# Product 3 of a sparse layer stack: rows gathered for three units at the start, then for the unit three ahead

## The chip, the cores and the metric

One Trainium2 chip, one of its cores. The metric is the device time in microseconds (us) of one execution; the lower the better. Beside it, one further execution was taken with the hardware profiler, and the views quoted below come from that one.

## The reference, cut to what matters

Four graph layers on 4096 nodes with 128 features share one adjacency matrix, and each ends in a residual sum and a layer norm. The matrix is sparse (about 0.2% of its entries are not zero), but it is given dense, as 64 MB of float32. The change lies in layer 1, a Chebyshev layer made of two convolutions with two products each by the matrix:

```python
def cheb_conv(x, L, W, b):
    Tx0 = x
    out = Tx0 @ W[0]
    Tx1 = L @ x
    out = out + Tx1 @ W[1]
    Tx2 = 2.0 * (L @ Tx1) - Tx0
    out = out + Tx2 @ W[2]
    return out + b
h = elu(cheb_conv(x, L, W0, b0))
h = elu(cheb_conv(h, L, W1, b1))
```

## The kernel before, in words

The adjacency matrix stays in HBM. It is read as chunks of 1 MB (4 x 128 rows by 512 columns) on SyncE's DMA queue, line 145, into a pool of five buffers. A product by the matrix is, for a block of 512 columns, eight chunks with four matmuls each (`propagate`, line 722, the matmul at line 730).

Layer 1 has four such products. They need the matrix four times over, and loading and multiplying it costs TensorE and DMA time. So the kernel finds the non-zero entries of each row while the chunks pass, and makes lists of them (`Lists.build`, line 1405, on VectorE). With a finished list a block of 512 result rows can be computed another way: the needed rows of the right-hand side are gathered one index per partition from a table in HBM, and weighed and summed on chip. In product 3 (`L @ h` with `h` already multiplied by a weight, called `v`), the blocks `PAIRED = [0, 1, 2]` are done that way, and the five blocks 3 to 7 are done densely by `propagate`.

The gathered part of product 3 is cut into 12 units of 128 result rows (`third_product`, line 1660). For a unit u:

- `pull(u)`, line 1665, takes a buffer `got3` of a pool with three buffers and issues nine gathers (`rows_of`, line 1543), each an indirect DMA on GpSimd of 128 rows of 512 bytes. Behind each stands `pause`, a multiplication of one column (line 1563). Both are tied, by `keep_in_program_order` (line 1518), behind the instruction written before them on GpSimd. That tie sets an order in GpSimd's queue and no wait for another engine.
- `weigh(u)`, line 1670, on ScalarE and VectorE: it scales the unit's own rows (line 1551), makes three one-hot matrices `hot` (line 1553) and adds six of the nine gathered rows, weighed, to `here` (line 1556).
- `product(u)`, line 1676, on TensorE: three matmuls of `hot` by the other three gathered rows (line 1682), two by a weight (line 1684), then the sum into `w` on VectorE (line 1685). In the kernel before, `pull(u + 2)` is written behind it.

When these are written is set by a plan with hooks: one hook for each of the 40 dense chunks. `weigh(u)` is written at hooks 6, 9, 11, 14, 16, 19, 22, 24, 27, 30, 32 and 35, and `product(u)` one hook later. At hooks 0 to 4 and at every odd one a step of `build` for the lists of blocks 3 to 7 is written (line 1715). Behind product 11, at hook 36, stand 24 gathers of list values (`values`, line 1521), and behind these on GpSimd the gathers for the next product (line 2006).

The order in which engines carry out what is written is, up to the end of product 3, set by the compiler's planner: on each engine it takes the instruction that is ready first by its own reckoning of durations, and among the ready ones the one written first. Exceptions are tied: gathers and pauses on GpSimd as said, and on VectorE everything of `build` and `weigh` in the order written (`chained`, line 1379). A new tile in a pool of three buffers waits at its first write for the last reader of the tile that had the buffer before. From `sparse_layers` (line 1722) on, the order on TensorE, VectorE, ScalarE and GpSimd is the order written.

Of the kernel before, what the change touches and what calls it, by code (L numbers as in the profile page):

```python
# [46 lines left out]
def adj_resnorm_d4(ctx: ExitStack, tc: tile.TileContext, x_in, xT_in, adj, adjT, pairs, diag_in, w0g, w0gT, a0, w1a, b1a,  # L47
# [633 lines left out]
    def network(usual):  # L681

        with ExitStack() as whole:
# [3 lines left out]
            with ExitStack() as first, ExitStack() as l1h_pool:  # L687
# [123 lines left out]
                if usual:  # L811
                    fetch(PAIRED[-1], TB * 9)
                    lists.paired(PAIRED[-1])
                    l1s = l1h_pool.enter_context(tc.tile_pool(name="l1s", bufs=2, reuse_waits="tile"))
                    third = third_product(lists, l1s, ps_tr, ps_mm, v, w, hT, W1B, wd, h0T)
# [774 lines left out]
    def tile_of(u):  # L1590
        return PAIRED[u // TB] * TB + u % TB
# [68 lines left out]
    def third_product(lists, pool, ps_tr, ps_mm, v, w, hT, W1B, wd, h0T):  # L1660
        units = len(PAIRED) * TB
        E = NEAR + QT
        got, made = {}, {}

        def pull(u):
            if u < units:
                got[u] = pool.tile([P, E, F], F32, name="got3", bufs=3)
                deque(lists.rows_of(u, got[u], 0), 0)

        def weigh(u):  # L1670
            here = pool.tile([P, F], F32, name="here3")
            hot = pool.tile([P, QT, P], F32, name="hot3")
            lists.weigh(u, v[:, tile_of(u), :], got[u], here, hot, True)
            made[u] = here, hot

        def product(u):
            t = tile_of(u)
            here, hot = made.pop(u)
            g = got.pop(u)
            p = ps_tr.tile([P, F], F32, name="ptr")  # L1680
            for j in range(QT):
                nc.tensor.matmul(p, hot[:, j, :], g[:, j, :], start=j == 0, stop=False)
            for hh in range(hT.shape[1]):
                nc.tensor.matmul(p, hT[:, hh, t * P:(t + 1) * P], W1B[:, hT.shape[1] + hh, :], start=False, stop=hh == hT.shape[1] - 1)
            nc.vector.tensor_tensor(w[:, t, :], p, here, ALU.add)
            pull(u + 2)
            if u % TB == TB - 1:
                c = PAIRED[u // TB]
                blk = slice(c * IB, (c + 1) * IB)
                lists.store(1, c, w)  # L1690
                ph = ps_mm.tile([P, IB], F32, name="pmm")
                for hh in range(hT.shape[1]):
                    nc.tensor.matmul(ph, wd[:, hh, :], hT[:, hh, blk], start=hh == 0, stop=hh == hT.shape[1] - 1)
                nc.scalar.copy(h0T[:, blk], ph)

        def builds():
            for c in (3, 4, 5, 6, 7):
                for _ in lists.build(c, True):
                    yield

        build = builds()
        pull(0)
        pull(1)
        plan = {}
        for u, h in enumerate((6, 9, 11, 14, 16, 19, 22, 24, 27, 30, 32, 35)):
            plan.setdefault(h, []).append(lambda u=u: weigh(u))
            plan.setdefault(h + 1, []).append(lambda u=u: product(u))
        plan[36].append(lambda: (deque(lists.values(3), 0), deque(lists.values(4), 0)))
        hooks = [0]

        def seen(ib, n, c, a):
            h = hooks[0]
            hooks[0] += 1
            if h < 5 or h % 2:
                next(build, None)
            for f in plan.pop(h, ()):
                f()
            if h == 39:
                assert not plan and next(build, None) is None
        return seen  # L1720
# [436 lines left out]
```

## Time and profile before

| what | value |
|---|---|
| time, median of 3 runs | 1839.98 us (1831.49 to 1844.66) |
| the profiled execution, its own time | 1653.07 us |
| its span, first to last instruction | 1651.2 us |
| granted TensorE clock, mean over the span | 0.95 |
| busy: TensorE, VectorE, GpSimd, ScalarE | 90%, 69%, 50%, 23% |
| product 3, about 808 to 1000 us: TensorE, VectorE, GpSimd busy | 181.19, 152.57, 147.74 of 192 us |
| HBM read | 404.39 MB, 253 GB/s with what is written |

The profiled execution was 187 us shorter than the median of the plain runs. It is one execution, and the page doesn't show a plain one; positions and durations below are those of the profiled execution.

Engines are called PE (TensorE), PEld (its weight loads), DVE (VectorE), ACT (ScalarE), POOL (GpSimd) and SP (SyncE). A line of the timeline has the start in us, the duration in us, engine, source line, operation, what is written and read, the count of merged instructions, and in brackets how long the engine sat idle before it and what released it ("issue": nothing that the profile shows). The trace writes `got` for the tile `got3` and `rows` for the table. The matmuls of float32 are recorded as two instructions each, so that three matmuls are "x6".

### The profile page before, as it was taken

To read this page: it belongs to the slowest core of one execution; us is meant where nothing else is said; L and a number is where in the kernel's file an instruction comes from. 1 tells how busy PE (TensorE), PEld (TensorE's weight loads), DVE (VectorE), ACT (ScalarE), POOL (GpSimd) and SP (SyncE) were. 2 spreads that over 40 slices of the span, in tenths; PEclk is the share of its full clock that TensorE was granted. 3 is DMA by queue.
4 is the path that set the end of the run, shared out by engine and by line. 5 is a ranking of instruction groups with operands and counts; after the bars stand their busy time and mean duration, and the time that the engine had idled before them with its cause. 6 is when DMAs were issued, how large, how long until landed. Compare 5 with 4: busy or idle time off the path is not lost.

```text
span 1651.2 us, 16460 instructions
## 1 busy us (share of the span) xinstructions
PE 1478.5 (90%) x4744; PEld 714.2 (43%) x4744; DVE 1138.4 (69%) x3203; ACT 385.5 (23%) x693; POOL 833.1 (50%) x1322
## 2 busy tenths in 40 slices
PE   6899999999999999999999999889927689788886
PEld 3344444544444444454444454444413344444444
DVE  5987655789887897988699950455336756556766
ACT  5776540010000011121200000222223111122234
POOL 0000000000242188848486888888648888888841
PEclk9999999999999999999999999999967798889988
DMA  9867776588888885867587888778665677678673
GB/s 374 342 256 301 246 271 233 179 277 299 316 315 320 309 285 195 281 210 274 177 296 248 291 278 305 252 265 287 241 151 153 189 259 244 219 239 278 218 192 95
DMA packets 106972, 419.30 MB, mean 254 GB/s; under 512 B 21556, under 2 KB 44088, under 8 KB 67064
## 3 DMA queue, kind: packets, MB, share of 16 engines
q1 hardware_dynamic: 59984, 360.01, 61.1%
q0 software_dynamic: 22656, 36.17, 8.6%
q10 hardware_dynamic: 24232, 21.98, 4.5%
q8 instruction: 39, 0.64, 0.2%
q14 instruction: 61, 0.50, 0.1%
HBM read 404.39 MB, written 13.70 MB: 253 GB/s over the span
## 4 chain that ended last, share of the span: by engine, by line
PE 46%; DVE 25%; POOL 14%; issue 6%; DMA 6%; ACT 3%; ACTq 0%; DVEq 0%; POOLq 0%
PE pacc L730 15%; PE pacc L423 12%; POOL got L1820 6%; PE pp L2050 5%; DMA got<-table,source 4%; PE pp L1931 3%; POOL got L1518 3%; DVE at L1397 3%; DVE top L1396 2%; POOL idle L1563 2%; DVE here L1556 1%; POOL value L1518 1%; DVE same L1317 1%; DVE gw L1856 1%; DVE acc L1944 1%
## 5 line engine op out<-in xcount | busy, mean ns | idle before, releaser
L1820 POOL DMA_INDIRECT got<-table,source x288 | 275.8, 958 | 88.8 <-issue 62.0
L1931 PE MATMUL pp<-chunk,xT 128*128 128x512 f32 x496 | 244.0, 633 | 1.4 <-ACT xT L1902 0.7
L730 PE MATMUL pacc<-chunk,x 128*128 128x512 f32 x512 | 222.6, 593 | 0.0
L1518 POOL DMA_INDIRECT got<-rows,source x180 | 182.8, 1016 | 67.6 <-issue 38.6
L423 PE MATMUL pacc<-chunk,hw 128*128 128x512 f32 x408 | 188.7, 607 | 0.8 <-DVE hw L466 0.7
L1358 POOL IOTA i<- 128x384 int32 (+3 forms) x4 | 1.0, 238 | 345.7 <-PE pden L411 329.8
L2050 PE MATMUL pp<-chunk,w 128*128 128x512 f32 x384 | 173.1, 600 | 0.0
L730 PE MATMUL pacc<-chunk,t 128*128 128x512 f32 x384 | 171.5, 597 | 0.0
L730 PEld LDWEIGHTS pacc<-chunk,x 128*128 128x128 f32 x512 | 96.0, 190 | 114.7 <-issue 114.6
L730 PE MATMUL pacc<-chunk,v 128*128 128x512 f32 x320 | 144.5, 597 | 0.0
L1396 DVE MAX8 top<-chunk 128x8 f32<-128x512 f32 x196 | 128.5, 677 | 14.1 <-DMA chunk<-in_adjT 14.1
L1931 PEld LDWEIGHTS pp<-chunk,xT 128*128 128x128 f32 x496 | 94.2, 203 | 91.2 <-issue 84.1
L1397 DVE FIND_INDEX8 at<-top,chunk 128x8 uint16<-128x512 f32 x196 | 133.1, 684 | 0.0
L1518 POOL DMA_INDIRECT both_ways<-in_pairs,both_at x108 | 106.6, 987 | 17.4 <-issue 17.1
L423 PEld LDWEIGHTS pacc<-chunk,hw 128*128 128x128 f32 x408 | 75.0, 192 | 92.1 <-issue 86.3
L1563 POOL TENSOR_TENSOR idle<-idle 128x1 f32<-128x1 f32 x489 | 110.3, 226 | 8.6
L730 PEld LDWEIGHTS pacc<-chunk,t 128*128 128x128 f32 x384 | 71.7, 192 | 81.8 <-issue 81.8
L2050 PEld LDWEIGHTS pp<-chunk,w 128*128 128x128 f32 x384 | 71.7, 194 | 78.5 <-issue 77.7
L395 ACT ACTIVATE junk<-chunk 128x2048 fp8e4<-128x2048 f32 x51 | 97.4, 1910 | 29.8 <-DMA chunk<-in_adjT 29.3
L329 DVE TENSOR_SCALAR pos<-chunk 128x2048 bf16<-128x2048 f32 x66 | 80.1, 1219 | 33.7 <-DMA chunk<-in_adjT 32.1
L1863 PE MATMUL u<-gw,into 128*128 128x132 f32 x192 | 33.2, 317 | 68.3 <-DVE gw L1856 68.3
L1556 DVE SCALAR_TENSOR_TENSOR here<-got,back,here 128x128 f32<-128x128 f32 x120 | 42.2, 352 | 67.0 <-DMA got<-rows,source 63.8
(424 smaller groups left out, 2058.7 us busy)
## 6 DMA issues: line engine op xcount, KB each, us to landing
chunk<-in_adjT SPq DMA_DIRECT2D x326, 1024.0 KB, 5.4
keep<-in_adjT SPq DMA_DIRECT2D x13, 1024.0 KB, 11.0
spread<-spread ACTq DMA_DIRECT2D x16, 384.0 KB, 4.5
got<-table,source POOLq DMA_INDIRECT x288
chunk<-in_adjT ACTq DMA_DIRECT2D x4, 1024.0 KB
got<-rows,source POOLq DMA_INDIRECT x180
table<-rows ACTq DMA_DIRECT2D x8, 264.0 KB, 5.2
xT<-in_xT ACTq DMA_DIRECT2D x8, 256.0 KB, 6.5
```

The lines of the kernel that those rows point to most:

```text
L329: r = nc.vector.tensor_scalar(pos, a, 0.0, None, op0=ALU.is_gt)
L395: nc.scalar.activation(junk, a, AF.Relu, scale=-1.0, accum_out=bad[:, n:n + 1], saturate=False)
L423: in_order(nc.tensor.matmul(p, hw[:, j * TB + k, :], a[:, k, :], start=first and k == 0, stop=last and k == TB - 1))
L730: nc.tensor.matmul(p, stationary(c * TB + k), a[:, k, :], start=n == 0 and k == 0, stop=n == NB - 1 and k == TB - 1)
L1396: pin(nc.vector.max(self.top[:, t, ib, :], row))
L1397: pin(nc.vector.max_index(self.at[:, t - TB, ib, :], self.top[:, t, ib, :], row))
L1518: tc.keep_in_program_order(nc.gpsimd.indirect_dma_start(out, None, of, bass.IndirectOffsetOnAxis(ap=index, axis=0)))
L1556: pin(nc.vector.scalar_tensor_tensor(here, got[:, j, 0:F], self.back[:, u, j:j + 1], here, op0=ALU.mult, op1=ALU.add))
L1563: return nc.gpsimd.tensor_tensor(self.idle[:, 0:1], of, self.idle[:, 1:2], ALU.mult)
L1820: nc.gpsimd.indirect_dma_start(got[t][:, j, :], None, table, bass.IndirectOffsetOnAxis(ap=lists.source[:, t, j:j + 1], axis=0))
L1931: nc.tensor.matmul(p, y[:, t0 + k, :], a[:, ib % (TB // n), k, :], start=k == 0, stop=k == n - 1)
L2050: nc.tensor.matmul(p, w[:, c * TB + k, :], a[:, k, :], start=n == 0 and k == 0, stop=n == NB - 1 and k == TB - 1)
```

## The change

At its beginning product 3 pulls the rows of units 0, 1 and 2 and not only of units 0 and 1; behind product u it pulls those of unit u + 3 and not of unit u + 2. The pool keeps its three buffers, `pull` still does nothing for a unit past the last, and the hooks, the lists and the number of gathers (108) stay.

```diff
@@ third_product, product(u)
             nc.vector.tensor_tensor(w[:, t, :], p, here, ALU.add)
-            pull(u + 2)
+            pull(u + 3)
             if u % TB == TB - 1:
@@ third_product
         build = builds()
-        pull(0)
-        pull(1)
+        for u in range(3):
+            pull(u)
         plan = {}
```

## The prediction, made before the changed kernel was run

> **What bounds the kernel now.** I read the page first, for the shares of the engines and for the rows of the gathers:
>
> ```profile
> span 1651.2 us, 16460 instructions
> ...
> PE 1478.5 (90%) x4744; PEld 714.2 (43%) x4744; DVE 1138.4 (69%) x3203; ACT 385.5 (23%) x693; POOL 833.1 (50%) x1322
> ...
> L1518 POOL DMA_INDIRECT got<-rows,source x180 | 182.8, 1016 | 67.6 <-issue 38.6
> ```
>
> TensorE is busy for 90% of the span, so over the whole it is the bound. The gathers on POOL take 1.016 us each, without the pause behind them. Then I asked for busy times by stage, of product 3 (808 to 1000 us) and of the begin of the next product (to 1110 us):
>
> ```profile
> 808.00:1000.00 192.00, 181.19 (x582) 87.00 (x581) 152.57 (x551) 12.74 (x26) 147.74 (x231) 1.00 0.80 272
> 1000.00:1110.00 110.00, 98.17 (x285) 48.34 (x284) 38.71 (x130) 17.55 (x33) 95.10 (x166) 0.95 0.80 273
> ```
>
> The columns are: the stretch, its length, then busy us and counts of PE, PEld, DVE, ACT and POOL, the clock, the DMA share and GB/s. PE leaves 192 - 181.19 = 10.8 us idle in product 3 and 110 - 98.17 = 11.8 us after it, and that is all that a better supply of rows could give back to PE there. The chain of waits for the same stretch puts POOL's gathers first (17.2% "POOL got L1518", 7.5% "POOL value L1518"), and it follows POOL without a gap from 965.77 us, a gather of product 3, to 1072.23 us, a gather of the next product. So POOL's stream does set when the rows arrive at the end of this stage. A gap in that stream before 965 us is not free.
>
> So the third view was the timeline of POOL, for the gaps, and beside it that of PE and DVE for who reads the buffers. First POOL:
>
> ```profile
> 855.18 0.97 POOL L1518 DMA_INDIRECT got<-rows,source  x1 [0.15 <-issue]
> 856.54 0.97 POOL L1518 DMA_INDIRECT got<-rows,source  x1 [0.15 <-DVE high L1317]
> 857.53 0.20 POOL L1563 TENSOR_TENSOR idle<-idle 128x1 f32<-128x1 f32 x1
> 861.02 0.97 POOL L1518 DMA_INDIRECT got<-rows,source  x1 [3.29 <-PE pacc L730]
> ...
> 872.06 1.20 POOL L1518 DMA_INDIRECT got<-rows,source  x1 [0.15 <-issue]
> 873.27 0.29 POOL L1563 TENSOR_TENSOR idle<-idle 128x1 f32<-128x1 f32 x1
> 886.10 0.97 POOL L1518 DMA_INDIRECT got<-rows,source  x1 [12.53 <-issue]
> ```
>
> and the first three products on PE and weighings on DVE, which are units 0, 1 and 2:
>
> ```profile
> 857.63 1.00 PE L1682 MATMUL ptr<-got,hot 128*128 128x128 f32 x6 [0.54 <-DVE hot L1553]
> 882.71 1.00 PE L1682 MATMUL ptr<-got,hot 128*128 128x128 f32 x6
> 890.00 0.83 PE L1682 MATMUL ptr<-got,hot 128*128 128x128 f32 x6
> ```
>
> ```profile
> 858.01 2.28 DVE L1556 SCALAR_TENSOR_TENSOR here<-got,back,here 128x128 f32<-128x128 f32 x6
> 883.08 2.28 DVE L1556 SCALAR_TENSOR_TENSOR here<-got,back,here 128x128 f32<-128x128 f32 x6
> ```
>
> The first gather of product 3 starts at 816.16 us. Counting nine to a unit, unit 0 is 816.16 to 829.43, unit 1 starts at 830.79, unit 2 at 843.00 and has its ninth at 856.54, unit 3 starts at 861.02 and has its ninth at 872.06, unit 4 starts at 886.10. What decides this case is to lay these starts beside the products behind which the pulls are written. Pull 2 is written behind product 0, but its first gather started at 843.00, 14.6 us before product 0 (857.63). Pull 3 is written behind product 1 (882.71) and started at 861.02, 21.7 us before it. Pull 4 is written behind product 2 (890.00) and started at 886.10. So the written place does not hold a gather back. What holds it is its buffer: unit 3 needs that of unit 0, whose last reader on DVE ended at 858.01 + 2.28 = 860.29, and the gather came 0.73 us later. Unit 4 needs that of unit 1, read until 883.08 + 2.28 = 885.36, and came 0.74 us later. Unit 2 found the third buffer free, since nobody had used it, and followed unit 1 with the usual 0.15 us.
>
> **What the Trainium skill says.** "PSUM — Partial Sum Buffer", section "Engine vs sequencer instructions", says that the queues of ScalarE, VectorE and GpSimd are strictly first in, first out. The trace agrees: while the first gather of unit 4 waits 12.53 us, nothing else runs on POOL. "DMA: Bandwidth & Descriptors", section "Issuing engine by pattern", gives indirect transfers to GpSimd, and its section "Latency and other measured facts" puts the first byte of a transfer from there at about 1 us; here the gather's instruction itself takes 0.97 us at the least. No price from it is used below.
>
> **The change part by part.**
>
> (1) Pull 2 moves from behind product 0 to the begin: nine gathers, nine pauses and one new buffer. All three buffers are free at that time, and no other work of POOL is written between pull 1 and the old place of pull 2 (the list building has none). So POOL's queue reads unit 0, 1, 2 in both kernels, and the gathers of unit 2 already start where the change asks for them. Gain 0, cost 0. No cover is used up for that: POOL does the same at the same time, from 843.00 to 857.7 us.
>
> (2) Pulls 3 to 11 move one product earlier, each with nine gathers and nine pauses, 81 of each. Again only POOL is concerned, again the queue's order stays unit by unit, and the list values at hook 36 stay behind unit 11. Each new place is directly behind the product that frees its buffer (unit u + 3 takes the buffer of unit u), and the wait for that buffer stays: 3.29 us before unit 3 and 12.53 us before unit 4. I followed the rule "start at the later of POOL being done and last DVE reader plus 0.74 us" through the rest. Units 5, 6, 7, 10 and 11 found the buffer free and started with the usual 0.15 us. Unit 8 started at 938.07 after 0.45 us idle (unit 5 was read until 937.33) and unit 9 at 953.18 after 0.69 us (unit 6 until 952.44). All nine obey it, and in none does the product written before the pull come in. Gain 0, cost 0. What would be worth something here is a fourth buffer or an earlier weighing of units 0 and 1, and the change brings neither: together the two large gaps are (3.29 - 0.15) + (12.53 - 0.15) = 15.5 us of POOL.
>
> (3) Waits. A gather of unit u + 3 waits for the readers of unit u before and after. What is queued behind it on POOL is the rest of the pulls, for which the weighings on DVE wait (in product 3 they sat idle 20.2 us for gathers, with the two waits of PE). No wait is added, none is removed. The 108 gathers, the chunk loads on SP's queue and the stores on ACT's stay the same in number; SP's queue is not passed, since the pulls stand on POOL alone.
>
> (4) The other engines. PE, DVE, ACT and SP carry the same instructions in the same relative written order, because only POOL's instructions move against them. The planner sees the same rows arrive at the same time, so I see no reason why it should set a product elsewhere. Cost 0; bounded by the rivals below from both sides.
>
> Sum: 1653.07 + 0 = 1653.07 us for the profiled execution, with a span of 1651.2 us and 1.9 us around it. The plain runs have a median of 1839.98 us, 11% more; what makes them longer no view shows. A change of nothing carries over whatever that is, so I predict 1840 us. Where a rival below has a price in the profile's us, I scale it by 1840/1653 = 1.113.
>
> **The rivals.** *Faster: the written place holds gathers after all*, for instance through the planner's reckoning, and units 3 and 4 start earlier once they are written earlier. For it speaks that POOL's stream carries the chain from 965.77 us on, so that each us won there could count. Against it speaks that both gaps end 0.73 and 0.74 us after the last reader of the buffer. At most the 15.5 us go: 1637.6 us in the profile, 1840 - 17 = 1823 us, 0.9% less. I give it and anything else that makes it faster 7 in 100, with 5 in 100 for over 1%.
>
> *Slower: the planner sets products earlier on PE*, because with the pulls written before the next list step it reckons their rows ready sooner. Then PE, which takes its instructions in turn, waits at a product whose rows are not there. The place is units 9 to 11, 963 to 992 us, where the rows come last: there and elsewhere DVE and PE sat idle 20.2 us for gathers, of which PE had only 0.9, since dense matmuls were placed before the products. If that cover goes, PE pays up to 20.2 - 0.9 = 19.3 us: 1672 us in the profile, 1840 + 21 = 1861 us, 1.2% more. It decides from the point where a product stands so early that fewer dense matmuls lie before it than its rows are late. Against it: the tie on POOL lets the gathers run at the same times, so the planner has nothing new to reckon with. 6 in 100, with 4 in 100 for over 1%.
>
> *The change does what it says and helps in vain*: rows would arrive earlier, but PE is 94% busy in product 3 (181.19 of 192), so at most its idle 10.8 us could go. It needs an earlier start of some gather, which (1) and (2) exclude; it lies within the first rival.
>
> **How the numbers follow.** No change 87 in 100, faster 7, slower 6. The first alone has the range of the three runs before, 1831.5 to 1844.7, made symmetric and a little wider for another median: 1830 to 1850. To hold 8 in 10 with the scatter of a second set of runs and some of both rivals I take 1826 to 1854. About 1% is what a measurement of this kernel can tell from no change. Over 1% faster: the 5 of the first rival and 1 for scatter, 0.06. Over 1% slower: 0.04 and 1 for scatter, 0.05. Within 1%: 0.89.
>
> **What would show it right or wrong.** Right: POOL's timeline after has unit 2 directly behind unit 1, again gaps of about 3 and 12 us before the 28th and 37th gather of product 3, and again 0.74 us from the last DVE reader to the gather; the same counts of instructions on each engine; PE and DVE in the same order. Wrong: a different place of the products at line 1682 among the dense matmuls of line 730, a gap before unit 2, other gaps before units 3 and 4, or PE waiting for gathers at line 1682 for much more than 0.9 us. If the time changes by over 1% while these views stay, the cause is outside what I have read.

## The result, and the profile after

| | median, us | runs |
|---|---|---|
| before | 1833.35 (1824.3 to 1852.43) | 22 |
| after | 1834.05 (1827.59 to 1847.12) | 22 |

The ratio after / before is 1.0003, with a 95% interval of 0.9987 to 1.0019: no difference. (The ratios here and below are taken over the fast runs and are not the quotients of the medians; the two differ by up to 0.0014.) The forecast was 1840 us with no change as the likeliest case.

The two compiled programs, laid side by side, say why: on each engine they hold the same instructions in the same order, with the same operands, addresses and waits. Only the numbers in the names of buffers and instructions and the references to source lines differ. The change moved text in the source and nothing on the chip.

This has to be kept in mind when the two profiles are compared. The page of after:

```profile
span 1843.7 us, 16456 instructions
PE 1537.3 (83%) x4740; PEld 734.9 (40%) x4744; DVE 1139.2 (62%) x3203; ACT 385.6 (21%) x693; POOL 830.2 (45%) x1322
L1518 POOL DMA_INDIRECT got<-rows,source x180 | 182.2, 1012 | 125.5 <-DVE rec L1317 49.0
```

The span is 192.5 us longer than that of before (1651.2 us), and that is not the change: the profile of before caught an execution in which TensorE was slowed for less of the time (granted clock 0.95, here 0.904) and which was shorter than all 22 plain runs of the same kernel, so the two profiles are compared by the order of events and not by their lengths. The counts agree: 1322 on POOL, 3203 on DVE, 693 on ACT, 4744 weight loads; of 4744 matmuls four have no record here. A gather takes 1.012 us (before: 1.016).

Product 3's first dense matmul starts in this profile at 876 us (before: 802 us); positions below called "past the begin of product 3" count from there. POOL's timeline around units 2, 3 and 4:

```profile
916.22 0.97 POOL L1518 DMA_INDIRECT got<-rows,source  x1 [0.15 <-issue]
917.22 0.20 POOL L1563 TENSOR_TENSOR idle<-idle 128x1 f32<-128x1 f32 x1
917.57 0.97 POOL L1518 DMA_INDIRECT got<-rows,source  x1 [0.15 <-issue]
...
931.23 0.35 POOL L1563 TENSOR_TENSOR idle<-idle 128x1 f32<-128x1 f32 x1
937.45 0.97 POOL L1518 DMA_INDIRECT got<-rows,source  x1 [5.88 <-PE ptr L154]
...
949.68 0.30 POOL L1563 TENSOR_TENSOR idle<-idle 128x1 f32<-128x1 f32 x1
962.52 0.97 POOL L1518 DMA_INDIRECT got<-rows,source  x1 [12.53 <-issue]
```

917.57 us is the first gather of unit 2, directly behind unit 1 as before. 937.45 and 962.52 us are the first gathers of units 3 and 4, each behind a gap. The products 0, 1 and 2 on PE, and the weighings of units 0 and 1 on DVE:

```profile
935.13 0.83 PE L1682 MATMUL ptr<-got,hot 128*128 128x128 f32 x6
959.13 1.00 PE L1682 MATMUL ptr<-got,hot 128*128 128x128 f32 x6
966.42 0.83 PE L1682 MATMUL ptr<-got,hot 128*128 128x128 f32 x6
```

```profile
934.43 2.28 DVE L1556 SCALAR_TENSOR_TENSOR here<-got,back,here 128x128 f32<-128x128 f32 x6
959.50 2.28 DVE L1556 SCALAR_TENSOR_TENSOR here<-got,back,here 128x128 f32<-128x128 f32 x6
```

The readers of unit 0 end at 934.43 + 2.28 = 936.71 us, and unit 3 starts 0.74 us later. Those of unit 1 end at 959.50 + 2.28 = 961.78 us, and unit 4 starts 0.74 us later. The name in the bracket (a transpose of PE at line 154) is merely the event nearest in time; the arithmetic names the reader. A third gap, 5.13 us before unit 8 at 1019.49 us (before: 0.45 us), ends 0.74 us after the last reader of unit 5 as well.

What does differ from the profile of before is the end of the stage. There POOL went from the last list value to the first gather of product 4 without a gap:

```profile
1021.35 0.97 POOL L1518 DMA_INDIRECT value<-in_adjT,where  x1 [0.15 <-issue]
1022.34 0.20 POOL L1563 TENSOR_TENSOR idle<-idle 128x1 f32<-128x1 f32 x1
1022.70 0.97 POOL L1518 DMA_INDIRECT got<-rows,source  x1 [0.15 <-issue]
```

In the profile of after POOL is through with its values and waits 23.12 us for the table `rows` to be stored from `w`, product 3's result:

```profile
1102.90 0.97 POOL L1518 DMA_INDIRECT value<-in_adjT,where  x1 [0.15 <-issue]
1103.89 0.20 POOL L1563 TENSOR_TENSOR idle<-idle 128x1 f32<-128x1 f32 x1
1127.22 0.97 POOL L1518 DMA_INDIRECT got<-rows,source  x1 [23.12 <-DMA rows<-w]
```

PE's timeline shows why `w` is late. Near the end of product 3's work PE falls to one matmul every 1.4 or 2.1 us for the most part, with nothing that the profile could name as the cause ("issue"):

```profile
1092.56 1.01 PE L1693 MATMUL pmm<-hT,wd 128*128 128x512 f32 x1 [0.38 <-issue]
1094.66 1.01 PE L730 MATMUL pacc<-chunk,v 128*128 128x512 f32 x1 [1.09 <-issue]
1096.09 1.01 PE L730 MATMUL pacc<-chunk,v 128*128 128x512 f32 x1 [0.41 <-issue]
...
1107.32 9.47 PE L730 MATMUL pacc<-chunk,v 128*128 128x512 f32 x16 [0.18 <-issue]
```

And by stretch (columns as in the prediction's table of windows):

```profile
1040.00:1066.00 26.00, 23.97 (x80) 12.09 (x79) 11.90 (x38) 1.68 (x4) 22.80 (x38) 1.00 0.47 154
1066.00:1071.00 5.00, 2.10 (x4) 0.56 (x3) 1.05 (x3) 0.00 (x0) 4.34 (x8) 1.00 0.51 164
1071.00:1107.00 36.00, 17.72 (x24) 6.59 (x23) 1.38 (x4) 0.00 (x0) 28.98 (x50) 0.50 0.14 45
1107.00:1119.00 12.00, 11.82 (x26) 5.01 (x25) 1.08 (x3) 1.17 (x2) 0.00 (x0) 0.79 0.89 350
```

In 41 us, 1066 to 1107, PE begins 27 matmuls (one of them is counted in two rows of the table); in the 26 us ahead of them it did 80. The DMA falls to 45 GB/s, and SyncE's queue of chunk loads waits 26.5 us for PE there; behind the stretch it is back at 350 GB/s. So it follows PE and does not lead. "TensorE: Matmul & The Clock Gate" of the Trainium skill, section "What's actually happening", says that the clock is halved after an idle window of about 3.4 us. The trace does not show that rule at work here: the pace drops at 1066 us under a clock of 1.00, PE then sits idle for 1.55 us at the longest, and yet 0.50 is granted from 1071 to 1112 us. What can be read is the order: the half clock comes behind the pacing and does not explain its begin. What sets the pace is in no view.

### The profile page after: what moved, and what is told of

Its sections match the earlier page's. It is cut to its first block, busy times and chain, and to the rows that moved or that the text cites. A ratio compares the mean times of both kernels' runs of the same rounds, so it can differ in the third digit from the quotient of the medians.

```text
span 1843.7 us, 16456 instructions
## 1 busy us (share of the span) xinstructions
PE 1537.3 (83%) x4740; PEld 734.9 (40%) x4744; DVE 1139.2 (62%) x3203; ACT 385.6 (21%) x693; POOL 830.2 (45%) x1322
## 4 chain that ended last, share of the span: by engine, by line
PE 49%; DVE 21%; another core or an unknown queue 10%; issue 9%; DMA 4%; ACT 3%; POOL 2%; DVEq 0%; ACTq 0%; POOLq 0%; SPq 0%
PE pacc L730 18%; PE pacc L423 10%; PE pp L1931 7%; PE pp L2050 3%; DVE at L1397 2%; DVE top L1396 2%; DMA got<-table,source 2%; DVE here L1556 1%; DVE spread L1317 1%; DVE acc L1944 1%; DVE gw L1856 1%; PE pden L411 1%; DVE same L1317 1%; DVE here L1858 1%
## 5 line engine op out<-in xcount | busy, mean ns | idle before, releaser
L1931 PE MATMUL pp<-chunk,xT 128*128 128x512 f32 x496 | 261.6, 671 | 9.8 <-issue 5.3
L730 PE MATMUL pacc<-chunk,t 128*128 128x512 f32 x384 | 189.0, 639 | 14.0 <-issue 14.0
L730 PE MATMUL pacc<-chunk,v 128*128 128x512 f32 x320 | 154.8, 623 | 9.5 <-issue 9.1
L1931 PEld LDWEIGHTS pp<-chunk,xT 128*128 128x128 f32 x496 | 100.2, 216 | 105.9 <-issue 96.6
L730 PEld LDWEIGHTS pacc<-chunk,t 128*128 128x128 f32 x384 | 76.9, 205 | 107.3 <-issue 107.2
L1944 DVE TENSOR_TENSOR acc<-pp,acc 128x512 f32<-128x512 f32 x96 | 62.4, 683 | 58.8 <-remote 35.9
L730 PEld LDWEIGHTS pacc<-chunk,v 128*128 128x128 f32 x320 | 60.2, 196 | 84.7 <-issue 84.7
```

Source lines behind the costliest of these rows:

```text
L730: nc.tensor.matmul(p, stationary(c * TB + k), a[:, k, :], start=n == 0 and k == 0, stop=n == NB - 1 and k == TB - 1)
L1931: nc.tensor.matmul(p, y[:, t0 + k, :], a[:, ib % (TB // n), k, :], start=k == 0, stop=k == n - 1)
L1944: nc.vector.tensor_add(acc3[:, blk], p, acc3[:, blk])
```

## The experiments

Two runs hold rows back on purpose (held2, two_buffers), one writes the pulls as late as possible (one_ahead), and one holds them in the kernel after (held3). The runs that follow look into the surprise of held3 (held3_again and all with "pause" in the name) or take out the gaps (weigh_early, weigh_early2). Each ratio is to before on the same chip in the same hour. The four sets of measurements ran on three chips, the second and the fourth on the same one; before itself had medians of 1836.35, 1840.92, 1809.7 and 1831.92 us in them, so times are compared inside a set only.

**held2**: make POOL really wait where the text of before only seemed to say so. A pause that reads `w` stands ahead of each pull.

```diff
+            if u + 2 < units:
+                tc.keep_in_program_order(lists.pause(w[:, t, 0:1]))
             pull(u + 2)
```

> The kernel before, with one multiplication of a column more on GpSimd ahead of each pull behind a product: it reads the first column of the rows of w that the product has just written, so that the gathers really wait for that product (pull u + 2 behind product u). Theory (the written place held nothing, the buffers did): now unit 2 starts only about 0.7 us after the sum of product 0, 18 us later than before, and the stream of gathers reaches unit 4 about 7 to 12 us later (893 to 898 us in place of 886 on the clock of the profile before); the time is 0.3 to 0.8% longer. Rival (the written place held the gathers already in the kernel before): the same starts as before, the time within 0.1%.

Measured: 1837.12 us, ratio 0.9991 (0.9972 to 1.001). The wait is there, with DVE's sum at line 1685 as its releaser:

```profile
935.20 0.19 POOL L1563 TENSOR_TENSOR idle<-w,idle 128x1 f32<-128x1 f32 x1 [18.87 <-DVE w L1685]
935.85 0.97 POOL L1518 DMA_INDIRECT got<-rows,source  x1 [0.45 <-issue]
```

Unit 2 starts at 935.85 us, 61 us past the begin of product 3 (after: 41), and unit 11 at 194 (after: 183). The starts came nearly as expected (unit 4 is 13 us later than in after, not 7 to 12) and the time did not: 11 us on POOL cost nothing, for they come out of the time that POOL waits for `rows` in the end, 9.52 us here and 23.12 us in after. A program in which the written place did hold the gathers would have had this profile; before and after do not have it.

**two_buffers**: before with a pool of two.

```diff
-                got[u] = pool.tile([P, E, F], F32, name="got3", bufs=3)
+                got[u] = pool.tile([P, E, F], F32, name="got3", bufs=2)
```

> The kernel before with two buffers got3 in place of three, pull u + 2 behind product u as before. Theory (buffers set the starts): unit 2 waits for the last reader of unit 0 and starts at about 861 and not 843 us on the clock of the profile before, unit 3 waits for unit 1 (886 and not 861), unit 4 follows at about 898 and not 886; the time is 0.3 to 0.8% longer. Rival (the written place sets the starts, and a kernel that asks two ahead never needs a third buffer): the time within 0.1%.

Measured: 1850.82 us, ratio 1.0072 (1.0044 to 1.01). The gathers of unit 2 now wait for the buffer of unit 0:

```profile
937.57 0.97 POOL L1518 DMA_INDIRECT got<-rows,source  x1 [19.75 <-PE ptr L154]
```

Units 3 and 4 start at 86 and 99 us past the begin, as expected. So the pool sets the start, as the prediction had it. The size of the loss (six runs) is in the expected range, but its reason is not shown: held2 starts units 2 to 4 just as late and loses nothing, and on DVE the compiled programs of the two differ in the order of two neighbouring instructions of this stage alone.

**one_ahead**: write the pulls as late as possible.

```diff
         pull(0)
-        pull(1)
...
-            pull(u + 2)
+            pull(u + 1)
```

> Three buffers as before, but only unit 0 is pulled at the begin and unit u + 1 behind product u. Theory: the written place of a pull holds nothing, so unit 2 still follows unit 1 and unit 1 unit 0 without a gap, and the time is within 0.2% of before. Rival (the written place counts): each unit is gathered in series with its weighing, about 12 us each for 11 units with at best half of it hidden, over 3% longer.

Measured: 1838.55 us, ratio 1.0003 (0.9984 to 1.0023). Its compiled program, too, is the same as that of before in every instruction. One, two or three units ahead in the text is one program.

**held3**: after, with a pause on `w` ahead of `pull(u + 3)`. The pool allows no earlier start anyway, so only the pauses themselves are new.

```diff
+            if u + 3 < units:
+                tc.keep_in_program_order(lists.pause(w[:, t, 0:1]))
             pull(u + 3)
```

> The changed kernel with the same hold: pull u + 3 behind product u, made to wait for the sum of product u. Theory: the hold asks for hardly more than the buffer already does (the last reader of unit u on VectorE), so unit 3 and each later one starts at most 0.7 us later than in the changed kernel and unit 2 directly behind unit 1; the time within 0.2% of before. Against the kernel with the hold and pull u + 2 it is 0.3 to 0.8% faster: that is what the change would have been worth if the place held the gathers. Rival: no difference between the two held kernels.

Measured: 1823.78 us, ratio 0.9928 (0.9901 to 0.9954), over seven runs. It is 0.7% faster than before, where no change was expected. Against held2 it is faster by about the expected 0.3 to 0.8%, but not for the expected reason, since held2 lost nothing. No gather starts earlier than in after by more than 0.3 us (units 2, 3, 4 and 11 at 41, 62, 87 and 183 us). The second set was for that.

**held3_again** is the same kernel once more; **spare_pause** has the nine pauses without the read of `w`, so without any wait.

```diff
+            if u + 3 < units:
+                tc.keep_in_program_order(lists.pause())
             pull(u + 3)
```

> The changed kernel with the hold (pull u + 3 waits for the sum of product u), the same program once more. It was 0.7% faster than the kernel before though it only adds nine small instructions and waits. Theory A (the hold changes when a stretch of slowed TensorE falls at the end of product 3, and does so each time): again 0.5 to 1% faster, product 3 about 223 us long in the profile and not 243. Theory B (that was chance of one set of seven runs): within 0.3% of before, product 3 about 243 us.

> The changed kernel with the same nine instructions more on GpSimd at the same places in its queue, but reading only their own column, so that none waits for a product. Theory A1 (the wait makes the difference): as the changed kernel, within 0.3%. Theory A2 (any small shift of GpSimd's stream by nine times about 0.35 us does): about 0.5 to 1% faster, like the held kernel.

Measured: 1826.14 us, 0.9923 (0.989 to 0.9956), and 1823.89 us, 0.9915 (0.9885 to 0.9944). The gain repeats (eight and six runs), and it needs no wait: the theory of the wait falls. Nine instructions of about 0.3 us that compute nothing make the kernel 0.8% faster here. Another plan of the compiler is not the reason: in the programs of held3, spare_pause, pause_first and pause_late, PE, DVE and ACT have the same instructions in the same order at the same addresses as in after. Only the pauses on POOL, and the counts of its work that others wait for, are new.

**pause_first** and **pause_late** put one such pause ahead of unit 3 alone, and four ahead of units 8 to 11.

```diff
+            if u + 3 == 3:
+                tc.keep_in_program_order(lists.pause())
             pull(u + 3)
```

```diff
+            if 8 <= u + 3 < units:
+                tc.keep_in_program_order(lists.pause())
             pull(u + 3)
```

> The kernel after with a single spare pause on POOL (about 0.3 us, it waits for nothing), ahead of the gathers of unit 3. That place is followed by POOL's wait for the buffer of unit 0 (3 us), so the pause moves no gather. Theory B1 (the nine spare pauses help by shifting the late gathers, up to the hand-over to product 4): no gain here, within 0.3% of before. Theory B2 (any other program with other instructions on POOL falls out differently, whatever the place): 0.7 to 0.9% faster again.

> The kernel after with four spare pauses on POOL, one ahead of each of units 8 to 11, none before. Theory B1 (late gathers shifted): most of the gain of the nine, 0.5 to 0.9% faster. If the early ones (units 3 to 7) carry the gain: within 0.3% of before.

Measured: 1812.0 us, 1.0022 (0.9999 to 1.0046), and 1807.71 us, 0.9989 (0.9967 to 1.0012). The first is as B1 had it, the second is a miss for B1. But this set, the only one on its chip, had a before of 1809.7 us, 1.5 to 1.7% under that of the sets of held3 and spare_pause. The last run therefore asks whether the pauses or the set made the difference.

**spare_pause_again**, in the fourth set, on the chip of the second:

> The kernel with nine spare pauses once more, since the three kernels with fewer pauses, or with the pauses and the earlier weighing, ran where before itself had 1810 us and showed at most 0.3%. Theory C1 (the gain belongs to the nine pauses): 0.7 to 1.0% faster again, whatever time before has. Theory C2 (the gain belongs to where the slowed stretch of TensorE falls in the one set of measurements): 0.7 to 1.0% where before has about 1835 to 1840 us, at most 0.4% where it has about 1810 us.

Measured: 1822.77 us against 1831.92, 0.9941 (0.992 to 0.9962). Faster again, by less than C1 or C2 had said. In three sets where before took 1832 to 1841 us the nine pauses gave 0.6 to 0.9%. That it is the nine and not four, or the set or its chip, is not decided: nine pauses without another edit were not run in the set of 1810 us.

**weigh_early**: take out the largest gap. Unit 1 is weighed at hook 6 and not 9, so that its buffer comes free for unit 4.

```diff
-        for u, h in enumerate((6, 9, 11, 14, 16, 19, 22, 24, 27, 30, 32, 35)):
+        for u, h in enumerate((6, 6, 11, 14, 16, 19, 22, 24, 27, 30, 32, 35)):
```

> The kernel before with unit 1 weighed at hook 6 in place of 9 (and its product at 7), so that its buffer is free about 20 us earlier; nothing else is moved. Theory (the gap of 12.5 us before unit 4 is the wait for unit 1's last reader): that gap goes, unit 4 starts about 72 us after the begin of product 3 and not 85, the later units up to 12 us earlier. Whether time follows: in the profile of the changed kernel the gathers after product 3 start some 20 us after GpSimd has done the list values, so GpSimd's stream is not what ends the stage in plain runs, and the time is within 0.4% of before. Rival (the stream of gathers carries the end of the stage, as the chain in the profile before had it): 0.5 to 0.8% faster.

Measured: 1833.96 us, 0.9948 (0.9927 to 0.997). Unit 4 starts at 74 us and not at 86, so the gap is gone, though a new one of 5.88 us stands before unit 5. The 0.5% lies at the low end of what the rival said, and the interval, 0.3 to 0.7%, reaches into both expectations: the run does not decide between them.

**weigh_early2** weighs all units earlier, at hooks 2, 3, 6, 8, 14, 16, 19, 22, 24, 27, 30 and 33.

> The kernel before with the units weighed at hooks 2, 3, 6, 8, 14, 16, 19, 22, 24, 27, 30 and 33, most one unit's step earlier. Theory: both gaps of GpSimd go (3.3 and 12.5 us), unit 4 starts about 70 us and unit 11 at most 165 us after the begin of product 3 in place of 85 and 183; weighings never free buffers late. The time within 0.5% of before where something else ends the stage; the rival that GpSimd's stream carries it expects 0.8 to 1.2% less.

Measured: 1838.55 us, 0.9994 (0.9971 to 1.0016). Unit 4 starts at 69 us, unit 11 at 178 (not at 165 as expected, for POOL waits 9.03 us before unit 7), and the time is that of before. Here earlier rows came without a gain, so the 0.5% of weigh_early can't be put down to them on this evidence. Both edits move weighings and products too, so the effect of the rows alone was not measured.

**pause_weigh** joins the nine pauses and the edit of weigh_early.

> The kernel after with the nine spare pauses and with unit 1 weighed at hook 6 instead of 9. If the two gains are of different kinds they add: 1.2 to 1.4% faster than before. If both only keep the same slowed stretch of TensorE out of product 3's dense matmuls: 0.5 to 0.9% faster, as one alone. A shift back into the slowed stretch would give no gain at all.

Measured, in the set of pause_first: 1801.88 us against 1809.7, 0.9969 (0.994 to 0.9998). That is none of the three cases expected, though the interval reaches into the second. Neither edit was run alone in this set, so whether their gains add is not shown.

What the shorter of the plain-length profiles have in common is where the slowed stretch falls. In us, from one profile each, the last column being POOL's idle time before that gather:

| kernel | product 3 | product 4 | both | first gather of product 4, after the begin of product 3 | idle before it |
|---|---|---|---|---|---|
| before | 199 | 243 | 442 | 221 | 0.15 |
| after | 243 | 248 | 491 | 251 | 23.12 |
| one_ahead | 242 | 244 | 486 | 248 | 21.76 |
| held2 | 244 | 241 | 485 | 248 | 9.52 |
| two_buffers | 251 | 246 | 497 | 260 | 15.93 |
| weigh_early | 234 | 250 | 484 | 240 | 15.97 |
| weigh_early2 | 229 | 256 | 485 | 245 | 22.13 |
| held3 | 223 | 243 | 466 | 228 | 0.15 |
| held3_again | 229 | 248 | 477 | 232 | 3.63 |
| spare_pause | 214 | 257 | 471 | 228 | 0.15 |
| spare_pause_again | 220 | 254 | 475 | 227 | 0.15 |
| pause_first | 231 | 245 | 476 | 240 | 15.96 |
| pause_late | 207 | 261 | 468 | 227 | 0.15 |
| pause_weigh | 205 | 261 | 466 | 223 | 0.15 |

(Lengths run from the first matmul of a product to that of the next.) The timeline of PE in pause_late, at the end of product 3 and in product 4, where line 2052 is the dense matmul of product 4:

```profile
1064.18 10.46 PE L730 MATMUL pacc<-chunk,v 128*128 128x512 f32 x24
...
1077.86 20.87 PE L2052 MATMUL pp<-chunk,w 128*128 128x512 f32 x48 [0.97 <-issue]
1099.20 1.13 PE L2052 MATMUL pp<-chunk,w 128*128 128x512 f32 x2 [0.47 <-issue]
1101.02 1.29 PE L2052 MATMUL pp<-chunk,w 128*128 128x512 f32 x2 [0.70 <-issue]
1103.82 1.29 PE L2052 MATMUL pp<-chunk,w 128*128 128x512 f32 x2 [1.51 <-issue]
1107.32 1.01 PE L2052 MATMUL pp<-chunk,w 128*128 128x512 f32 x1 [2.21 <-issue]
```

Product 3 ran through at full pace, and the slow matmuls begin at 1099 us, behind it. In after they lay at 1066 to 1107 us, within it. So the stretch falls at different places, and what product 3 wins (243 to 207 us) product 4 gives back in part (248 to 261 us). In held3's profile the stretch falls on the hand-over, where PE has only a few matmuls to do:

```profile
1076.33 1.02 PE L831 MATMUL pmm<-hT,wd 128*128 128x512 f32 x2
1088.14 1.11 PE L154 MATMUL ptr<-ident,t2T 128*128 128x128 f32 x4 [10.79 <-issue]
```

This is a reading of one profile per kernel, and the profiled executions exaggerate: that of after took 1845.46 us, the second longest of its 22, that of held3 1810.93 us, the shortest of its seven. pause_first, pause_late and pause_weigh come from the set in which before, too, was shorter. That the pauses shift the stretch is therefore a guess; what starts it stays open.

## Why the prediction was right, point by point

*Step (1), pull 2 moves to the begin: gain 0.* Right. Unit 2 is directly behind unit 1 in after (917.57 us, 0.15 us idle), 17.6 us ahead of product 0 (935.13 us), as before it was 14.6 us ahead. one_ahead, which writes it later still, is the same program.

*Step (2), pulls 3 to 11 move by one product: gain 0.* Right, and for the reason given. The gap before unit 3 was forecast at about 3 us and is 5.88, that before unit 4 at about 12 us and is 12.53; the rule of 0.74 us from the last reader on DVE holds at both. The first is larger because in that execution DVE ended unit 0 at 936.71 us, 5.13 us after POOL was through with unit 2 (931.58 us), where before it was 2.56 us (860.29 and 857.73 us). two_buffers shows the rule from the other side.

*Steps (3) and (4), no wait and no order changes.* Right to the instruction: the two programs are identical. With that the rival of the planner (1861 us) and that of the written place (1823 us) fall together. The planner had nothing new to reckon with, as the argument against the slower rival said.

*The sum.* 0 us, measured as a ratio of 1.0003. The forecast of 1840 us was the median of three runs; with 22 it is 1833.35 us.

*What was not right.* The prediction said that POOL's stream "does set when the rows arrive at the end of this stage" and that "A gap in that stream before 965 us is not free". This holds in the profile of before. In that of the same program taken as after, with the length of the plain runs, `w` comes last and POOL has 23 us to spare; held2's 11 us were free. Length alone does not decide it: in five other profiles of plain length, those with product 3 at 223 us or less, POOL again goes on after 0.15 us. What failed there is the step from one execution to all. The sentence on what would help ("a fourth buffer or an earlier weighing of units 0 and 1") is not borne out either: weigh_early took out the 12.53 us gap and gave 0.5%, weigh_early2 started units 3 to 11 earlier by 5 to 18 us than after's profile has them and gave nothing (both moved weighings too), and spare_pause, with both gaps in place, gave 0.85% in the same set. A fourth buffer was not tried: there is no room for it in SBUF beside the kernel's other tiles. Neither had a part in the sum, since the sum did not use the price of a gap.

The prediction also left open what makes the plain runs 11% longer. The later profiles, which have their length, show in part where it lies, though not why: of the 192.5 us between the two profiles of the identical program, 74.5 lie ahead of product 3, 43.8 in it, 5.3 in product 4 and 68.9 behind it. In product 3 it is for the most part the stretch shown above: at the pace of 80 matmuls in 26 us its 27 matmuls would take about 9 us and not 41 (an estimate, since their sizes differ).

## What to carry to other kernels

Before costing a moved prefetch, lay the start of its transfers beside the place where it is written. If they start ahead of that place, and behind the last reader of their buffer by a constant (0.73 to 0.74 us here), the pool sets the start and the text does not: moving the text within one engine's own order is then no change at all, and comparing the two compiled programs says so without a run. Which engine ends a stage is another matter: POOL's wait at the end of this one was 0.15 us in one profile and 23.12 us in another of the identical program, so take order and waits from one profile, but not that. And a gain under 1% proves no mechanism where nine idle pauses bring as much.

## What the runs showed of the hardware

One core's TensorE, with nothing to wait for in the profile, falls for about 40 us to one matmul every 1.4 or 2.1 us for the most part (27 matmuls in 41 us in after), first at clock 1.00 and from 5 us on at 0.50, and then takes up its pace again. Nine pauses of about 0.3 us each on GpSimd changed the time of the whole by 0.6 to 0.9% in three sets of measurements on two chips. Both were unexpected, and neither is explained here.
